# A graph kernel's counting one-hots in sets of four slots, its stream buffers released through ScalarE, its passes begun later

## The chip, the cores and the metric

The kernel runs on one core of a Trainium2 chip. The metric is the time of one execution in microseconds (us) on the device. The kernel before takes 1678.33 us, the median of three runs (1674.64 to 1681.06).

## The reference

12,500 nodes of 128 features pass a layer norm and a ReLU. 200,000 edges, sorted by destination, each bring the row of their source, multiplied by one of four weight matrices (by the edge's type) plus a bias, to their destination; the sums are added to x.

```python
h = jnp.maximum(_layernorm(x, axis=-1), 0.0)
xs = h[src]
msgs = jnp.zeros((xs.shape[0], W.shape[2]), dtype=x.dtype)
for i in range(4):
    mask = (edge_type == i)[:, None]
    msgs = msgs + jnp.where(mask, xs @ W[i] + b[i], 0.0)
out = x + jax.ops.segment_sum(msgs, dst, num_segments=12500)
```

The destinations are drawn so that low-numbered nodes have many edges and most nodes have few.

## The kernel before, in words

**The table.** In the first 190 us the kernel normalizes x and writes h to a table `htab` in DRAM, each row as three bf16 parts of 128 values whose sum is the fp32 value (lines 431 to 514). Row p·98 + j of the table is partition p, column j: `NW` is 98 columns.

**Dense nodes.** The first `C0` = 512 chunks of 128 edges belong to the nodes with many edges. For these the kernel does not fetch rows of h. It counts, for each node and type, how often each of the 12,500 rows occurs, and multiplies the table by these counts. The nodes come in units of three, whose counts share one 32-bit number as three bytes, and the units in batches of `UB` = 27 (18 batches, the first with 17 units).

- *Counting*, `count`, lines 935 to 987. A unit has 2 to 6 *slots*, each of up to 128 edges of one node. In batches 1 to 13 the first three or four units have 6 slots and the others 2; there are 1167 slots, 66 or 70 in most batches. For each slot VectorE (DVE) makes two one-hots, `o1` (128 x 128: which partition, lines 947 or 951) and `o2` (128 x 392: which column and type, line 952), and TensorE (PE) multiplies them into the unit's counts in a PSUM bank `pt` (line 963). After the last slot of a unit ScalarE (ACT) casts the bank into `counts` (line 966). One-hots are made `AHEAD` = 8 slots ahead of their matmul, in 12 buffers of each kind; each matmul waits for its own pair, and each making waits for the matmul that used the buffer last.
- *The pass* over the table, `multiply`, lines 989 to 1040. For each batch the whole table is streamed through SBUF in blocks of `HB` = 4 columns (384 KB, line 997, issued by SyncE, SP), with 4 buffers `hs`. For each column three matmuls (line 1001, one for each bf16 part) add into one PSUM bank `pa`, of which there is a single buffer. At the end ScalarE copies the sums out (`sd`, line 1011), and the next pass may write `pa`. A `tail` of four matmuls with the weights (line 1015) and the adds to the result follow a little later.
- *Their order*, `dense_work`, lines 1062 to 1091. The count of batch b+1 and the pass of batch b are written out side by side: whichever has done the smaller share goes next, and the pass is held as if `BEHIND` = 0.06 further on, so that 4 or 5 slots are counted before its first matmul and its last 6 or 7 columns have no slots beside them. The last pass has no counting beside it.
- `check_sums`, lines 968 to 985, is ten small DVE operations at the end of each count, which verify byte totals; all are issued at once.

**Sparse chunks.** The other 1051 chunks are handled in groups of 16. GpSimd (POOL) fetches their rows of `htab` by indirect DMAs (line 543, into buffers `hm` of the pool `rows`, 18 of them, two chunks each). DVE makes small one-hots `oh` (line 560), PE adds up rows by type (line 577), ScalarE copies the sums (`sb`, line 580), PE applies the weights and counts of biases (lines 595 and 604), and DVE adds the result to a ring of 2048 destination columns (line 665). Filled parts of the ring leave through a PE transpose (line 690), an add to x, fetched by SP (`xo`, line 676), and a store by SP (line 697).

**What sets the order.** The order of instructions on PE, DVE and ACT is that of the program, written out by hand (line 1270). `pace` (lines 1047 to 1057) spreads the dense work evenly over the parts of the sparse groups by TensorE columns. SP and POOL too execute in program order. The framework puts in the waits between engines. A wait that another one already implies is left out: an instruction that waits for a ScalarE copy does not also wait for the PE work that the copy waited for. `held_by` (line 516) adds a wait of one instruction for another by hand.

Of the kernel before, what the change touches and what calls it, by code (L numbers as in the profile page):

```python
# [35 lines left out]
F32 = mybir.dt.float32  # L36
BF16 = mybir.dt.bfloat16
# [5 lines left out]
ALU = mybir.AluOpType  # L43
# [5 lines left out]
P = 128  # L49
# [6 lines left out]
C0 = 512  # L56
UB = 27
MANY = 16
HB = 4
AHEAD = 8  # L60
HOTS = AHEAD + 4
BEHIND = 0.06
RING = 2048
OT = 4
HG = 2
# [8 lines left out]
def kernel(  # L74
# [10 lines left out]
    nc = tc.nc  # L85
# [144 lines left out]
    flag = const.tile([P, 1], I32, name="flag")  # L230

    mid = ExitStack()
    hpool = mid.enter_context(tc.tile_pool(name="rows", bufs=18))
    opool = mid.enter_context(tc.tile_pool(name="onehots", bufs=2))
    spool = mid.enter_context(tc.tile_pool(name="typed", bufs=2))
    x_ps = mid.enter_context(tc.tile_pool(name="x_ps", bufs=4, space=PSUM))
# [279 lines left out]
    def held_by(one, by, reason):  # L516
        tc.add_manual_dep(
            one.ins,
            by.name,
            mybir.DependencyInfo(mybir.DependencyClass.Sync, mybir.DependencyReason.DATA),  # L520
            reason=reason,
        )
# [409 lines left out]
            nc.scalar.copy(acc[:, a:z], pn[:, : z - a])  # L932


    def count(vs, counts):
        todo = []
        for i, u in enumerate(vs):
            of = slots_of(u)
            todo += [(i, c, by, n == 0, n == len(of) - 1) for n, (c, by) in enumerate(of)]
        made = {}  # L940

        def make(k):
            i, s, by, first, last = todo[k]
            o1 = op1.tile([P, P], BF16, name="o1")
            o2 = o2s[:, k % HOTS, :]
            if by == 1.0:
                nc.vector.tensor_scalar(o1, iota_1, loT[:, s : s + 1], None, ALU.is_equal)  # L947
            else:
                if by is None:
                    by = byT[:, (s - PAIRS) // 2 : (s - PAIRS) // 2 + 1]  # L950
                nc.vector.tensor_scalar(o1, iota_1, loT[:, s : s + 1], by, ALU.is_equal, ALU.mult)  # L951
            nc.vector.tensor_scalar(o2[:, :NB], iota_n, hkT[:, s : s + 1], None, ALU.is_equal)  # L952
            made[k] = o1, o2

        done = 0
        for k, (i, s, by, first, last) in enumerate(todo):
            while done < min(k + 1 + AHEAD, len(todo)):
                make(done)
                done += 1
            o1, o2 = made.pop(k)  # L960
            if first:
                pb = x_ps.tile([P, NB + NT], F32, name="pt")
            nc.tensor.matmul(pb, o1, o2, start=first, stop=last)  # L963
            if last:

                nc.scalar.copy(counts[:, :, i * NT : (i + 1) * NT], pb.rearrange("p (b t) -> p b t", t=NT))  # L966
            yield (k + 1) / len(todo)
        def check_sums():
            n = len(vs)
            bi = sdp.tile([P, UB], I32, name="bi")  # L970
            nc.vector.tensor_copy(bi[:, :n], counts[:, NW, : n * NT].rearrange("p (i t) -> p i t", t=NT)[:, :, 0])
            bb = sdp.tile([P, 3, UB], I32, name="bb")
            nc.vector.tensor_single_scalar(bb[:, 0, :n], bi[:, :n], 255, op=ALU.bitwise_and)
            nc.vector.tensor_single_scalar(bb[:, 2, :n], bi[:, :n], 16, op=ALU.arith_shift_right)
            nc.vector.tensor_single_scalar(bi[:, :n], bi[:, :n], 8, op=ALU.arith_shift_right)
            nc.vector.tensor_single_scalar(bb[:, 1, :n], bi[:, :n], 255, op=ALU.bitwise_and)
            bf = sdp.tile([P, 3, UB], F32, name="bf")
            nc.vector.tensor_copy(bf[:, :, :n], bb[:, :, :n])
            top = sdp.tile([P, 2], F32, name="top")
            nc.vector.tensor_reduce(top[:, 0:1], bf[:, :, :n], AX.XY, ALU.max)  # L980
            nc.vector.tensor_reduce(top[:, 1:2], bf[:, :, :n], AX.XY, ALU.add)
            nc.vector.tensor_max(most, most, top[:, 0:1])
            nc.vector.tensor_add(held, held, top[:, 1:2])

        tails.append(check_sums)

    tails = []

    def multiply(vs, counts):
        nu = len(vs)  # L990

        counts = counts.bitcast(F8)
        pa = a_ps.tile([P, 512], F32, name="pa")
        for j0 in range(0, NW, HB):
            j1 = min(j0 + HB, NW)
            hs = hsp.tile([P, HB, D3], BF16, name="hs")
            nc.sync.dma_start(hs[:, : j1 - j0, :], htab.rearrange("(p j) f -> p j f", j=NW)[:, j0:j1, :])
            for j in range(j0, j1):
                of = counts[:, j, : nu * NT * 4].rearrange("p (v m) -> p m v", m=4)[:, :3, :]
                for c in range(3):  # L1000
                    nc.tensor.matmul(  # L1001
                        pa[:, : 3 * nu * NT].rearrange("p (m v) -> p m v", m=3),
                        hs[:, j - j0, c * D : (c + 1) * D],
                        of,
                        start=(j == 0 and c == 0),
                        stop=(j == NW - 1 and c == 2),
                    )
                if j + 1 < NW:
                    yield (j + 1) / NW
        sd = sdp.tile([P, 3 * UB * NT], F32, name="sd")  # L1010
        nc.scalar.activation(sd[:, : 3 * nu * NT], pa[:, : 3 * nu * NT], AF.Copy, scale=512.0)  # L1011
        def tail():
            py = x_ps.tile([P, 3 * UB], F32, name="pt")
            for t in range(NT):
                nc.tensor.matmul(  # L1015
                    py[:, : 3 * nu],
                    wsb[:, t, :],
                    sd[:, : 3 * nu * NT].rearrange("p (v t) -> p v t", t=NT)[:, :, t],
                    start=(t == 0),
                    stop=(t == NT - 1),  # L1020
                )

            def rest():
                for m in range(3):
                    i = 0
                    while i < nu:
                        if vs[i][m] is None:
                            i += 1
                            continue
                        k, d = vs[i][m]  # L1030
                        by = 2 if m < 2 and k == 0 and d >= PAIRS else 1
                        n = next((e for e in range(1, nu - i) if vs[i + e][m] != (k, d + e * by)), nu - i)
                        to = acc[:, d : d + (n - 1) * by + 1 : by]
                        nc.vector.tensor_tensor(to, to, py[:, m * nu + i : m * nu + i + n], ALU.add)
                        i += n

            tails.append(rest)

        tails.append(tail)
        yield 1.0  # L1040
# [201 lines left out]
    counting = mid.enter_context(ExitStack())  # L1242
    dense = counting.enter_context(tc.tile_pool(name="dense", bufs=2))
    sdp = counting.enter_context(tc.tile_pool(name="sdp", bufs=1))
    op1 = counting.enter_context(tc.tile_pool(name="op1", bufs=AHEAD + 4))
    op2 = counting.enter_context(tc.tile_pool(name="op2", bufs=1))
    o2s = op2.tile([P, HOTS, NB + NT], BF16, name="o2")
    nc.vector.memset(o2s[:, :, NB:], 1.0)
    hsp = counting.enter_context(tc.tile_pool(name="hsp", bufs=4))
    raw_sums = outp.tile([P, OT, D], F32, name="xo").rearrange("p j d -> p (j d)")[:, : RAW * G * win_raw]  # L1250
    nc.scalar.copy(raw_sums, raw_py[:, : RAW * G * win_raw])
    raw_adds = [
# [19 lines left out]
    for gi, (t0, g) in list(enumerate(zip(starts, sizes)))[RAW:]:  # L1272
# [16 lines left out]
        for j, part in enumerate(sum_up(t0, g, *now, gi >= FULL)):  # L1289
            late, tails[:] = list(tails), []  # L1290
            while work and spent < pace(gi, part):
                spent = next(work, None)
                if spent is None:
                    work = None
            for f in late:
                f()
            if j == 0:
                if finish:
                    next(finish[0])
                if gi < final:  # L1300
                    oh, made = one_hots_of(starts[gi + 1], sizes[gi + 1])
                    side += made
            if j == when:
                if finish:
                    next(finish.pop(0))
                side.append(lambda: [ending.pop(0)() for _ in list(ending)])
                side += adds
                adds.clear()
                todo = min(todo, len(side) * parts // max(1, parts - 1 - j))
            left = todo * (parts - 1 - j) // parts - (0 if j >= when else todo - len(side))  # L1310
            while side and len(side) > left:
                side.pop(0)()
            for _ in range(2):
                if leaving:
                    leaving.pop(0)()
        assert not side
        if work is None and not dense_out:
            while tails:
                tails.pop(0)()
            dense_out = True  # L1320
            assert goes[0] < gi

# [161 lines left out]
```

## Time and profile before

| | |
|---|---|
| time, median of 3 runs (lowest, highest) | 1678.33 us (1674.64, 1681.06) |
| profiled execution: its time, its span | 1684.81 us, 1683.1 us |
| mean granted TensorE clock in it | 0.95 |
| stretch with counting, passes and sparse groups together | 190 to 1640 us |
| in that stretch: PE busy, DVE, ACT, POOL | 1275.7, 895.2, 330.6, 918.4 us |
| in that stretch: granted clock, DMA share, GB/s | 0.98, 0.65, 192 |
| matmuls of the passes (L1001), counting (L963), sparse (L577) | 5292, 1167, 3009 |

The profile page gives busy times of each engine, the course of the span in 40 slices, the chain of work that ended last, and the costliest groups of instructions by line. PE is TensorE's matmuls and PEld its weight loads beside them; SPq is SyncE's queue; L997 means line 997. Matmuls are pipelined, so the mean length of one in the profile is longer than the distance between two starts. In a group, "<-" and an engine names what ended the idle time before its instructions, and "issue" stands where no event in the profile explains it.

### The profile page before, as it was taken

What the parts mean: (1) busy time and instruction counts of PE and PEld (TensorE: products, weight loads), DVE (VectorE), ACT (ScalarE), POOL (GpSimd) and SP (SyncE); (2) the same over time, 40 slices, a digit from 0 to 9 for tenths busy, and PEclk for the clock granted to TensorE, in tenths of its full rate; (3) what the DMA queues carried; (4) which work ended last, traced back from release to release, by engine and by line L of the source; (5) the groups of instructions that cost most, each with busy time, mean ns of one, the idle gap of its engine ahead of it and who ended that gap; (6) DMA issues with size and microseconds to landing.
All of it is one profiled execution on the core that took longest, in us unless ns stands there. A gap on an engine that the chain in (4) does not pass through costs nothing.

```text
span 1683.1 us, 32652 instructions
## 1 busy us (share of the span) xinstructions
PE 1420.6 (84%) x10984; PEld 926.8 (55%) x10984; DVE 1033.9 (61%) x5305; ACT 445.3 (26%) x1095; POOL 1026.0 (61%) x1078
## 2 busy tenths in 40 slices
PE   3768589898889988888989888988888988898885
PEld 1336366555565556555656555655555555565554
DVE  7880677665766566576647566656654756565244
ACT  5593231222212122212221222122222222222111
POOL 7436666666666566666665666666656666666561
PEclk9875699999999999999999999999999999999997
DMA  7543376766666666666666666666656666666662
GB/s 225 158 155 82 88 233 207 205 199 193 201 190 194 190 196 191 203 193 183 197 194 183 185 196 183 191 201 187 188 165 193 203 187 191 181 194 186 198 185 68
DMA packets 157498, 308.92 MB, mean 184 GB/s; under 512 B 28202, under 2 KB 81116, under 8 KB 157325
## 3 DMA queue, kind: packets, MB, share of 16 engines
q1 hardware_dynamic: 107645, 204.99, 40.3%
q0 software_dynamic: 49680, 101.81, 21.3%
q8 instruction: 86, 1.41, 0.4%
q14 instruction: 87, 0.71, 0.1%
HBM read 290.65 MB, written 16.04 MB: 182 GB/s over the span
## 4 chain that ended last, share of the span: by engine, by line
PE 77%; issue 10%; DVE 5%; another core or an unknown queue 3%; ACT 2%; DMA 2%; SPq 1%; DVEq 0%; ACTq 0%
PE pa L1001 45%; PE pt L963 12%; PE ps L577 7%; PE py L604 6%; PE pt L1015 1%; DMA hs<-htab 1%; PE ps L634 1%; PE py L595 1%; PE pt L690 1%; DVE stt L439 1%; ACT h L460 1%; DVE o L952 1%; DMA hm<-in_x_dram 1%; DVE oh L560 1%
## 5 line engine op out<-in xcount | busy, mean ns | idle before, releaser
L543 POOL DMA_INDIRECT hm<-htab,srcT x1003 | 970.2, 967 | 580.3 <-issue 225.4
L1001 PE MATMUL pa<-counts,hs 128*128 128x324 fp8e4 (+1 forms) x5292 | 976.1, 305 | 112.9 <-issue 95.8
L1001 PEld LDWEIGHTS <-hs 128*128 128x128 bf16 x5292 | 494.2, 97 | 396.0 <-issue 167.9
L963 PE MATMUL pt<-o,o 128*128 128x396 bf16 x1167 | 383.5, 338 | 45.8 <-issue 39.1
L952 DVE TENSOR_SCALAR o<-iota_n,hkT 128x392 bf16<-128x392 f16 x1167 | 386.2, 331 | 14.0 <-PE pa L1001 5.5
L966 ACT CAST counts<-pt 128x396 int32<-128x396 f32 x476 | 229.4, 494 | 506.5 <-PE pt L963 204.4
L560 DVE TENSOR_SCALAR oh<-iota_b,keyT 128x56 bf16<-128x56 bf16 (+8 forms) x1003 | 169.3, 259 | 265.4 <-PE pt L963 88.1
L580 ACT COPY sb<-ps 128x224 f32<-128x224 f32 (+8 forms) x251 | 99.6, 397 | 531.2 <-PE pt L963 182.9
L665 DVE TENSOR_TENSOR ring<-ring,py 128x14 f32 (+7 forms) x976 | 167.5, 172 | 102.5 <-issue 21.5
L577 PE MATMUL ps<-oh,hm 128*128 128x56 bf16 (+8 forms) x3009 | 192.2, 197 | 29.3 <-issue 28.6
L951 DVE TENSOR_SCALAR o<-iota,loT 128x128 bf16<-128x128 bf16 x644 | 169.7, 264 | 75.2 <-PE pt L963 27.8
L577 PEld LDWEIGHTS <-hm 128*128 128x128 bf16 x3009 | 164.7, 98 | 89.5 <-issue 43.7
L951 DVE TENSOR_SCALAR o<-iota,loT,byT 128x128 bf16<-128x128 bf16 x417 | 136.1, 326 | 81.4 <-PE pt L963 40.9
L963 PEld LDWEIGHTS <-o 128*128 128x128 bf16 x1167 | 113.2, 98 | 95.3 <-issue 43.8
L604 PE MATMUL py<-sb,wsb 128*128 128x224 f32 (+7 forms) x488 | 128.6, 404 | 3.5 <-issue 3.2
L604 PEld LDWEIGHTS py<-sb,wsb 128*128 128x128 f32 x488 | 87.3, 191 | 28.5 <-issue 6.8
L527 POOL DMA_INDIRECT hx<-in_x_dram,srcT x48 | 50.2, 1045 | 39.4 <-DVE stt L439 13.9
L599 ACT CAST cnt<-py 128x224 bf16<-128x224 f32 (+7 forms) x61 | 24.0, 394 | 96.4 <-PE pt L963 29.2
L460 ACT ACTIVATE h<-hm,nmrt,rstdt 128x128 f32<-128x128 f32 x98 | 42.8, 495 | 3.5 <-DMA hm<-in_x_dram 2.6
L489 PE MATMUL ps<-h,ident 128*128 128x384 f32 (+1 forms) x34 | 18.1, 618 | 17.7 <-ACT h L460 14.6
L947 DVE TENSOR_SCALAR o<-iota,loT 128x128 bf16<-128x128 bf16 x106 | 26.8, 253 | 8.5 <-remote 4.2
L1015 PE MATMUL pt<-sd,wsb 128*128 128x81 f32 (+1 forms) x144 | 25.4, 334 | 2.7 <-ACT sd L1011 2.7
(234 smaller groups left out, 623.2 us busy)
## 6 DMA issues: line engine op xcount, KB each, us to landing
hs<-htab SPq DMA_DIRECT2D x432, 384.0 KB
hm<-htab,srcT POOLq DMA_INDIRECT x1003
htab<-h SPq DMA_DIRECT2D x32, 288.0 KB
xo<-in_x_dram SPq DMA_DIRECT2D x23, 256.0 KB
out_dram<-xo SPq DMA_DIRECT2D x23, 256.0 KB
hm<-in_x_dram SPq DMA_DIRECT2D x18, 192.0 KB
hs<-htab SPq DMA_DIRECT2D x18, 192.0 KB
hm<-in_x_dram SPq DMA_DIRECT2D x14, 168.0 KB
```

The costliest lines, as they stand in the source:

```text
L460: return nc.scalar.activation(h, xt(k), AF.Relu, bias=nmr[:, k : k + 1], scale=rstd[:, k : k + 1]).ins
L543: one = nc.gpsimd.indirect_dma_start(out=hm[:, (i - h0) * D3 : (i - h0 + 1) * D3], out_offset=None, in_=htab, in_offset=bass.IndirectOffse ...
L560: nc.vector.tensor_scalar(oh[:, i, :], iota_b[:, :K], keyf[:, at : at + 1], None, ALU.is_equal)
L577: nc.tensor.matmul(ps[:, i - i0, :], rows(i, c), oh[:, i, :], start=(c == 0), stop=(c == 2))
L580: nc.scalar.copy(sb[:, i0:i1].rearrange("p g t n -> p g (t n)"), ps[:, : i1 - i0, :])
L604: nc.tensor.matmul(py[:, :g, :], wsb[:, t, :], sb[:, :g, t, :], start=False, stop=(t == NT - 1))
L665: nc.vector.tensor_tensor(to, to, of(i), ALU.add)
L951: nc.vector.tensor_scalar(o1, iota_1, loT[:, s : s + 1], by, ALU.is_equal, ALU.mult)
L952: nc.vector.tensor_scalar(o2[:, :NB], iota_n, hkT[:, s : s + 1], None, ALU.is_equal)
L963: nc.tensor.matmul(pb, o1, o2, start=first, stop=last)
L966: nc.scalar.copy(counts[:, :, i * NT : (i + 1) * NT], pb.rearrange("p (b t) -> p b t", t=NT))
L1001: nc.tensor.matmul(pa[:, : 3 * nu * NT].rearrange("p (m v) -> p m v", m=3), hs[:, j - j0, c * D : (c + 1) * D], of, start=(j == 0 and c == 0),
```

## The change

- One-hots lie in four buffers of four slots each (16 slots instead of 12). A unit's slots are cut into pieces of at most four, and pieces are put together into sets as long as four are not exceeded. PE waits once for a set, at its first matmul, until the last one-hot of the set is made. DVE waits once per set, at its first one-hot, for the last matmul of the set that used the buffer. `o2` is made before `o1`. The sets are made two sets ahead at the start, and then one slot of the set after next for each matmul.
- Blocks of the table's stream have five columns (480 KB) instead of four, in 3 buffers instead of 4, so a pass has 20 blocks instead of 25. The DMA that fills a buffer is held, in addition, by a ScalarE copy of counts: of the copies that were written out after the buffer's last reader and before this DMA, the first. `left_at` keeps the copies with the number of blocks finished when they were written out. With no such copy the framework's wait for PE stays.
- `BEHIND` goes from 0.06 to 0.15.
- The pool `rows` has 16 buffers instead of 18.
- `check_sums` becomes a generator, of which each part of a sparse group takes one step.

```diff
-HB = 4
-AHEAD = 8
-HOTS = AHEAD + 4
-BEHIND = 0.06
+HB = 5
+SLOTS = 4
+SETS = 4
+STREAM = 3
+BEHIND = 0.15
...
-    hpool = mid.enter_context(tc.tile_pool(name="rows", bufs=18))
+    hpool = mid.enter_context(tc.tile_pool(name="rows", bufs=16))
...
+    left_at = []
+    by_blocks = [0]
+    released = []
+
     def count(vs, counts):
...
+            for one in [of[n : n + SLOTS] for n in range(0, len(of), SLOTS)]:
+                if not sets or len(sets[-1]) + len(one) > SLOTS:
+                    sets.append([])
+                sets[-1] += one
+        before = len(released)
+        released.extend(None for _ in sets)
+
+        def make(n):
+            at = before + n
+            o1 = op1.tile([P, SLOTS, P], BF16, name="o1")
+            o2 = o2s[:, at % SETS]
+            for k, (i, s, by, first, last) in enumerate(sets[n]):
+                one = nc.vector.tensor_scalar(o2[:, k, :NB], iota_n, hkT[:, s : s + 1], None, ALU.is_equal)
+                if k == 0 and at >= SETS:
+                    held_by(one, released[at - SETS], "a set of slots has been counted as a whole")
...
+                yield o1[:, k], o2[:, k], one.ins
...
+        for n, of in enumerate(sets):
+            while len(making) < min(n + 3, len(sets)):
+                making.append(make(len(making)))
+                made.append([])
+            for m in range(n, min(n + 2, len(sets))):
+                made[m] += list(making[m])
+            for k, (i, s, by, first, last) in enumerate(of):
+                if n + 2 < len(sets) and len(made[n + 2]) < len(sets[n + 2]):
+                    made[n + 2].append(next(making[n + 2]))
+                o1, o2, _ = made[n][k]
+                if first:
+                    pb = x_ps.tile([P, NB + NT], F32, name="pt")
+                one = nc.tensor.matmul(pb, o1, o2, start=first, stop=last)
+                if k == 0:
+                    held_by(one, made[n][-1][2], "a set of slots is counted when all of it is made")
+                if k == len(of) - 1:
+                    released[before + n] = one.ins
+                if last:
+                    one = nc.scalar.copy(counts[:, :, i * NT : (i + 1) * NT], pb.rearrange("p (b t) -> p b t", t=NT))
+                    left_at.append((by_blocks[0], one.ins))
...
     def multiply(vs, counts):
...
-            nc.sync.dma_start(hs[:, : j1 - j0, :], htab.rearrange("(p j) f -> p j f", j=NW)[:, j0:j1, :])
+            one = nc.sync.dma_start(hs[:, : j1 - j0, :], htab.rearrange("(p j) f -> p j f", j=NW)[:, j0:j1, :])
+            free = [by for n, by in left_at if n > by_blocks[0] - STREAM]
+            if free and by_blocks[0] >= STREAM:
+                held_by(one, free[0], "the buffer of the stream is free")
+            del left_at[: len(left_at) - len(free)]
...
+                if j + 1 == j1:
+                    by_blocks[0] += 1
...
-    op1 = counting.enter_context(tc.tile_pool(name="op1", bufs=AHEAD + 4))
+    op1 = counting.enter_context(tc.tile_pool(name="op1", bufs=SETS))
...
-    o2s = op2.tile([P, HOTS, NB + NT], BF16, name="o2")
-    nc.vector.memset(o2s[:, :, NB:], 1.0)
-    hsp = counting.enter_context(tc.tile_pool(name="hsp", bufs=4))
+    o2s = op2.tile([P, SETS, SLOTS, NB + NT], BF16, name="o2")
+    nc.vector.memset(o2s[:, :, :, NB:], 1.0)
+    hsp = counting.enter_context(tc.tile_pool(name="hsp", bufs=STREAM))
...
+            if checks and next(checks[0], None) is None:
+                checks.pop(0)
```

More of the change, by code (lines that the diff above doesn't have):

```diff
@@ L932, in make_slots @@
             nc.scalar.copy(acc[:, a:z], pn[:, : z - a])
+    left_at = []
+    by_blocks = [0]
+    released = []
     def count(vs, counts):
         todo = []
+        sets = []
         for i, u in enumerate(vs):
             of = slots_of(u)
[L939 to L953, printed above, removed]
@@ L955, in count @@
-        done = 0
-        for k, (i, s, by, first, last) in enumerate(todo):
-            while done < min(k + 1 + AHEAD, len(todo)):
-                make(done)
-                done += 1
[L960 to L967, printed above, removed]
+            of = [(i, c, by, n == 0, n == len(of) - 1) for n, (c, by) in enumerate(of)]
@@ new lines, in count @@
+            todo += of
+            for one in [of[n : n + SLOTS] for n in range(0, len(of), SLOTS)]:
[12 more added lines that the diff above has]
+                    held_by(one, released[at - SETS], "a set of slots has been counted as a whole")
+                if by == 1.0:
+                    one = nc.vector.tensor_scalar(o1[:, k], iota_1, loT[:, s : s + 1], None, ALU.is_equal)
+                else:
+                    if by is None:
+                        by = byT[:, (s - PAIRS) // 2 : (s - PAIRS) // 2 + 1]
+                    one = nc.vector.tensor_scalar(o1[:, k], iota_1, loT[:, s : s + 1], by, ALU.is_equal, ALU.mult)
+                yield o1[:, k], o2[:, k], one.ins
@@ new lines, in count @@
+        making = []
+        made = []
+        done = 0
+        for n, of in enumerate(sets):
[18 more added lines that the diff above has]
+                    left_at.append((by_blocks[0], one.ins))
+                done += 1
+                yield done / len(todo)
+            made[n] = None
@@ L971, in check_sums @@
             nc.vector.tensor_copy(bi[:, :n], counts[:, NW, : n * NT].rearrange("p (i t) -> p i t", t=NT)[:, :, 0])
+            yield True
             bb = sdp.tile([P, 3, UB], I32, name="bb")
@@ L974, in check_sums @@
             nc.vector.tensor_single_scalar(bb[:, 2, :n], bi[:, :n], 16, op=ALU.arith_shift_right)
+            yield True
             nc.vector.tensor_single_scalar(bi[:, :n], bi[:, :n], 8, op=ALU.arith_shift_right)
             nc.vector.tensor_single_scalar(bb[:, 1, :n], bi[:, :n], 255, op=ALU.bitwise_and)
+            yield True
             bf = sdp.tile([P, 3, UB], F32, name="bf")
             nc.vector.tensor_copy(bf[:, :, :n], bb[:, :, :n])
+            yield True
             top = sdp.tile([P, 2], F32, name="top")
@@ L981, in check_sums @@
             nc.vector.tensor_reduce(top[:, 1:2], bf[:, :, :n], AX.XY, ALU.add)
+            yield True
             nc.vector.tensor_max(most, most, top[:, 0:1])
             nc.vector.tensor_add(held, held, top[:, 1:2])
-        tails.append(check_sums)
+        checks.append(check_sums())
     tails = []
+    checks = []
     def multiply(vs, counts):
@@ L1319 @@
                 tails.pop(0)()
+            for check in checks:
+                for _ in check:
+                    pass
             dense_out = True
```

## The prediction

> **What bounds it now.** I read the busy shares and the granted clock first, then the chain that ended last, then the costliest groups.
>
> ```profile
> PE 1420.6 (84%) x10984; PEld 926.8 (55%) x10984; DVE 1033.9 (61%) x5305; ACT 445.3 (26%) x1095; POOL 1026.0 (61%) x1078
> ...
> PEclk9875699999999999999999999999999999999997
> ...
> PE 77%; issue 10%; DVE 5%; another core or an unknown queue 3%; ACT 2%; DMA 2%; SPq 1%; DVEq 0%; ACTq 0%
> ...
> L1001 PE MATMUL pa<-counts,hs 128*128 128x324 fp8e4 (+1 forms) x5292 | 976.1, 305 | 112.9 <-issue 95.8
> L963 PE MATMUL pt<-o,o 128*128 128x396 bf16 x1167 | 383.5, 338 | 45.8 <-issue 39.1
> L952 DVE TENSOR_SCALAR o<-iota_n,hkT 128x392 bf16<-128x392 f16 x1167 | 386.2, 331 | 14.0 <-PE pa L1001 5.5
> ...
> hs<-htab SPq DMA_DIRECT2D x432, 384.0 KB
> ```
>
> TensorE has 84% of the span and 77% of the last chain, so time is won only where it stands. In the dense stretch (190 to 1640 us) starts lie 143 ns apart for L1001 and 166 for L963; a table column (three L1001 with the counting and sparse matmuls between) takes .78 us, one without counting some .61. The waits of PE put 95.8 us before L1001 on "issue". Much of that is at one place per pass, its start. The timeline of one of them (start, length, engine and line; in brackets the idle time before and what ended it):
>
> ```profile
> 721.10 0.59 PE L1001 MATMUL pa<-counts,hs 128*128 128x324 fp8e4 x3
> 721.54 1.00 PE L963 MATMUL pt<-o,o 128*128 128x396 bf16 x5
> ...
> 725.19 0.45 ACT L1011 ACTIVATE sd<-pa 128x324 f32<-128x324 f32 x1
> ...
> 725.68 1.02 PE L1001 MATMUL pa<-counts,hs 128*128 128x324 fp8e4 x6 [3.15 <-issue]
> ```
>
> The old pass ends at 721.7, five slots follow, ScalarE copies the sums out only at 725.2, and the new pass (one `pa`) starts right behind. Over the 16 boundaries with counting, last to first L1001 is 3.59 us in the mean (.9 to 6.9). In each, L1001 follows the copy (.44 us), which starts 2.9 us after the last matmul did. So ScalarE learns late what PE has done: by about 3 us, also in mid-pass (last slot of a unit to its copy: mean 3.1 us, 80% between 1.55 and 4.55). In the before kernel block 0 has landed .3 to 3.8 us before the old pass ends, so the stream costs nothing there.
>
> What a stream block costs when it is waited for shows once in the chain:
>
> ```profile
> 1264.73 0.02 SPq L997
> 1264.75 0.03 issue
> 1264.78 3.84 DMA hs<-htab
> 1268.62 0.47 issue
> 1269.09 0.60 PE pa L1001 x3
> ```
>
> That is 3.8 us for 384 KB; in the mean the packets take 2.76 us and the last signal comes at 3.1. A 192 KB block takes 2.3. On that line 480 KB takes about 3.5 us (estimate).
>
> **The change, part by part.**
>
> *Sets of four slots.* 321 sets replace 1167 single waits of PE on DVE and some 840 of DVE on PE, and about 1000 of PE's 2650 semaphore updates go. PE's price: L1001 with an update starts its successor after 144 ns, without one after 143; so 0. DVE's lead falls from 8–9 slots to 4–8; a set is made in some 4 x 2 x .3 = 2.4 us, against 4 slots x 1.2 us = 4.8 us of PE per set, but DVE learns of a release 2–5 us late, and behind its waiting o2 stand the sparse one-hots (L560) and ring adds, for which L577 waits. Below 0, nothing; above, .05 us on each of 321 sets, 15 us. I take +5.
>
> *Pass starts.* BEHIND .15 puts 10–11 slots ahead of the first matmul instead of 4–5, so 5–6 x .166 = .9 us of counting (and .3 of sparse matmuls) moves into the gap. Against that stands the new hold. When block 0 of a pass is issued, `left_at` is asked for copies made after block B−3 ended. The old count's last copy is emitted near column 83, one block too soon; the first that qualifies is the new count's, and its first unit has 6 slots (batches 1–13; 3–4 after). So blocks 0, 1 and 2 wait on SP for a copy behind six slots and behind the sums' copy on ScalarE: with T0 the old pass's last matmul, 2.9 + .44 + .5 (L966, 494 ns) + .1 to issue = 3.9, then 3.5 to land: first L1001 at T0 + 7.5 against 3.59. Less 1.2 of useful work moved there: +2.7 us x 16 = **+43**. Were ScalarE not late, T0 + 1.3 + .5 + .1 + 3.1 = 5.0 and about +4 in all; with an exposed landing of 4.3, +56. I take 43: the lateness is in every boundary of the trace. Behind SP's hold stand the fetch of `xo` (L676) and the stores (L697), with groups of slack.
>
> *Clock.* Eight of the seventeen boundaries are followed by a slow stretch of 3.4 to 6.8 us. In the windows (start; width, PE, PEld, DVE, ACT and POOL busy, granted clock, DMA share, GB/s):
>
> ```profile
> 726.00:731.00 5.00, 5.00 (x30) 3.43 (x29) 4.60 (x26) 0.49 (x1) 2.97 (x4) 0.66 0.52 153
> 884.00:891.00 7.00, 5.96 (x22) 3.94 (x23) 7.00 (x40) 0.93 (x2) 3.07 (x3) 0.51 0.60 171
> 900.00:1100.00 200.00, 176.94 (x1419) 115.57 (x1417) 125.97 (x645) 46.15 (x110) 127.81 (x133) 0.99 0.65 192
> ```
>
> A stretch at half clock costs at least half of 3.4, 1.7 us. Idle gaps near 6 us should bring it at six more boundaries: **+10** (0 to 15). The Trainium skill (TensorE: Matmul & The Clock Gate, Part 1: The HAM clock gate) gives a window of about 3.4 us in which an idle TensorE falls to half rate; the 0.51 agrees, and by that rule alone every boundary would pay, which adds some 4 us to the sum.
>
> *Block 3 of a pass.* It needs a copy after block 0's end: that of slot 18, emitted at column 10 or 11; it is used at column 15, 4–5 columns or 3.1–3.9 us on. It needs 3.1 (ScalarE) + .5 + .1 + 3.5 = 7.2. Short by up to 3.7 us in the 13 batches with 6-slot units: at most 48, at least .3 x 13 = 4. Half: **+24**, since a pass that began late has PE waiting anyway.
>
> *Other blocks.* Three buffers of five columns are fewer (15 columns, not 16), and a release is seen on the next copy: every two slots, 2.3 us, so 1.16 later in the mean. A block needs 1.16 + 7.2 = 8.4 us from its predecessor's end to its use; two blocks of PE last 2 x 3.88 = 7.76. If strictly so, a block takes 4.18, +.3 us x 14 blocks x 17 passes = 71; if PE's pauses on issue (.1 us in each us) cover it, 0. Today a block's first use is 7.4 us after its issue in the median, so most landings hide with room. I take 40%: **+28**.
>
> *Rest.* `rows` from 18 to 16 buffers: each holds two chunks, so a group of 16 fills half of them instead of 8 of 18; POOL is 61% busy; 0 to 5, taken +2. The check's ten DVE operations (1.9 us a batch) spread over parts: off the path, −5 to 0, taken 0. The column count, matmuls and gathers stay.
>
> **Sum.** 43 + 10 + 5 + 24 + 28 + 2 = +112 us against the profiled execution's 1684.8 (span 1683.1). That run lies 6.5 over the median of 1678.3; I add the difference to the median: **1790 us**. Low ends 4 + 0 + 0 + 4 + 0 − 5 = +3; high ends 56 + 15 + 15 + 48 + 71 + 5 = +210. They will not all fall one way: 1740 to 1850 for this case.
>
> **Rivals.**
> 1. *Only the pass starts pay* (43 + 7): PE's pauses hide the rest. For it: landings hide 7.4 us ahead today. Against: two buffers' time is shorter than the need. 1728 us. Chance .12.
> 2. *The ring of three limits every block:* 43 + 10 + 48 + 71 + 7 = +179, about 1860. For it: the hold is in series with the landing. Against: the 90% of blocks issued over 5.3 us ahead today. .12.
> 3. *Faster:* PE's pauses are the price of its semaphore traffic. If L1001's 95.8 us scale with updates, 1000 of 2650 fewer give −36; more slots in the gaps add 16 x .9 = −14; and fewer long gaps give back some slow stretches. It decides if ScalarE's lateness shrinks with the updates from 3 us to below 1, so that block 0 lands within the gap. With two thirds of it, about 1645. Against: in the last pass, without counting and with half of the updates, the lateness is no shorter (3–5 us), and pauses go on at the same rate:
>
> ```profile
> PE pa L1001 <- issue: 5.7, 9, 1.0
> ```
>
>    (that pass's 66 us; in 1300 to 1500 it is 12.1 in 200). Chance .15. The Trainium skill (same page, "The cost: per-tile semaphore tail") prices each increment at 26.3 ns, one after another: 1000 fewer would be −26 us by it, which speaks for this rival; the 143 and 144 ns above do not show it.
> 4. *It doesn't do what it says:* the hold is never later than the old wait on PE, and gains and losses cancel. Against: block 0 now goes out before the old pass ends and then cannot. 1680 us, .06.
>
> The forecast has .55. About 0.5% (8 us) is what a measurement can tell from no change. Faster .15 (rival 3), the same .06, slower .79. The range, 1660 to 1880, leaves out half of rival 3 and the top of rival 2.
>
> **What would show it.** Pass boundaries near 7.5 us with L1001 waiting on DMA hs, not on the sums' copy; SP's L997 waiting on ACT L966; blocks 0–2 issued together behind the first copy of a batch; a wait at column 15; more windows near 0.5. Wrong if block 0 lands before the sums are copied, if the lateness of PE's signals falls with their number (then boundaries near 5 us), or if L1001's issue pauses shrink by a third.

## The result, and the profile after

The changed kernel takes 1745.21 us (median of 4, 1744.29 to 1748.43) beside 1676.49 us of the kernel before (median of 4): a ratio of 1.041, 95% interval 1.038 to 1.044, or +69 us. The profiled execution took 1744.29 us, its span is 1742.5. Lines move: the passes' matmuls are L1040, counting L985, the copy of counts L991, the stream's DMA L1032, the copy of the sums L1052. From the page of the changed kernel:

```profile
PE 1435.4 (82%) x10984; PEld 938.3 (54%) x10984; DVE 1015.9 (58%) x5305; ACT 450.0 (26%) x1095; POOL 1031.1 (59%) x1078
...
PEclk8976799998999899999999999999999899999997
...
PE 52%; issue 19%; DMA 14%; DVE 5%; another core or an unknown queue 4%; ACT 4%; SPq 2%; DVEq 0%; ACTq 0%
...
L1040 PE MATMUL pa<-counts,hs 128*128 128x324 fp8e4 (+1 forms) x5292 | 970.4, 309 | 195.1 <-DMA hs<-htab 150.7
...
hs<-htab SPq DMA_DIRECT2D x342, 480.0 KB
```

The work is the same, and PE's busy time nearly so. What is new is DMA: 14% of the chain instead of 2%, and 150.7 us of idle time before the passes' matmuls end with a block of the table, where before the largest releaser was "issue" with 95.8. The waits of PE and of SP's queue say the same from both ends (what waited, releaser, total, times, longest), first in the kernel before, then in the changed kernel:

```profile
PE pa L1001 <- issue: 95.8, 143, 4.6
...
PE pa L1001 <- DMA hs<-htab: 1.9, 3, 0.9
...
SPq L997 <- PE pt L963: 420.3, 150, 8.2
```
```profile
PE pa L1040 <- DMA hs<-htab: 150.7, 88, 8.1
PE pa L1040 <- issue: 40.3, 46, 4.6
...
SPq L1032 <- ACT counts L991: 633.3, 146, 12.1
```

SP now waits mostly for the copies of counts, where it waited for PE. But look at the lines on issue: while waits for blocks rose from 1.9 to 150.7 us, the pauses on issue fell from 95.8 to 40.3. This is the puzzle of the case.

The start of the same pass as in the prediction, in the changed kernel's timeline:

```profile
748.05 0.59 PE L1040 MATMUL pa<-counts,hs 128*128 128x324 fp8e4 x3
748.48 1.67 PE L985 MATMUL pt<-o,o 128*128 128x396 bf16 x9
...
749.74 0.44 ACT L1052 ACTIVATE sd<-pa 128x324 f32<-128x324 f32 x1 [0.36 <-PE pt L985]
...
750.51 0.49 ACT L991 CAST counts<-pt 128x396 int32<-128x396 f32 x1 [0.32 <-PE pt L985]
751.02 1.27 SPq L1032 DMA_DIRECT2D hs<-htab  x3
755.26 0.99 PE L1040 MATMUL pa<-counts,hs 128*128 128x324 fp8e4 x3 [4.60 <-issue]
```

Three DMAs go out together right behind the first copy of the new count, and PE starts 4.2 us after the first of them. The bracket on the last line says "issue", not DMA: the releaser is a guess from events, and the order of the lines tells more than the label. Column 15 of another pass:

```profile
601.64 0.49 ACT L991 CAST counts<-pt 128x396 int32<-128x396 f32 x1 [5.62 <-PE ps L578]
...
602.16 1.06 SPq L1032 DMA_DIRECT2D hs<-htab  x2
...
605.46 0.74 PE L1040 MATMUL pa<-counts,hs 128*128 128x324 fp8e4 x4 [2.70 <-DMA hs<-htab]
```

ScalarE stands idle for 5.6 us before the copy that lets block 3 go; the block is needed before it can have landed.

Two windows, over the start of one pass and of another (columns as in the prediction; the granted clock is third from the end):

```profile
588.00:593.00 5.00, 4.39 (x18) 3.11 (x19) 3.76 (x21) 0.49 (x1) 0.96 (x1) 0.50 0.54 213
1353.00:1358.00 5.00, 5.00 (x25) 3.76 (x26) 2.04 (x17) 0.00 (x0) 1.38 (x2) 0.50 0.75 258
```

PE counts as fully busy in the second and starts only 25 matmuls in 5 us: at half clock two L1040 start 269 ns apart instead of 143.

### The profile page after: what moved, and what is told of

Its sections match the earlier page's. It is cut to its first block, busy times and chain, and to the rows that moved or that the text cites. A ratio compares the mean times of both kernels' runs of the same rounds, so it can differ in the third digit from the quotient of the medians.

```text
span 1742.5 us, 32539 instructions
## 1 busy us (share of the span) xinstructions
PE 1435.4 (82%) x10984; PEld 938.3 (54%) x10984; DVE 1015.9 (58%) x5305; ACT 450.0 (26%) x1095; POOL 1031.1 (59%) x1078
## 4 chain that ended last, share of the span: by engine, by line
PE 52%; issue 19%; DMA 14%; DVE 5%; another core or an unknown queue 4%; ACT 4%; SPq 2%; DVEq 0%; ACTq 0%
PE pa L1040 27%; DMA hs<-htab 14%; PE pt L985 8%; PE py L605 5%; PE ps L578 4%; ACT counts L991 2%; PE pt L1056 2%; SPq L1032 1%; PE ps L635 1%; DVE oh L561 1%; PE py L596 1%; PE pt L691 1%; DVE o L967 1%; ACT sb L581 1%
## 5 line engine op out<-in xcount | busy, mean ns | idle before, releaser
L1040 PE MATMUL pa<-counts,hs 128*128 128x324 fp8e4 (+1 forms) x5292 | 970.4, 309 | 195.1 <-DMA hs<-htab 150.7
L1040 PEld LDWEIGHTS <-hs 128*128 128x128 bf16 x5292 | 490.9, 98 | 478.1 <-DMA hs<-htab 187.3
L959 DVE TENSOR_SCALAR o<-iota_n,hkT 128x392 bf16<-128x392 f16 x1167 | 381.3, 327 | 97.7 <-PE pt L985 44.1
L985 PE MATMUL pt<-o,o 128*128 128x396 bf16 x1167 | 374.9, 345 | 23.2 <-issue 10.4
L991 ACT CAST counts<-pt 128x396 int32<-128x396 f32 x476 | 230.0, 493 | 555.8 <-PE pt L985 306.3
L666 DVE TENSOR_TENSOR ring<-ring,py 128x14 f32 (+7 forms) x976 | 171.2, 175 | 82.5 <-PE py L605 20.8
L967 DVE TENSOR_SCALAR o<-iota,loT 128x128 bf16<-128x128 bf16 x644 | 175.2, 272 | 0.0
L985 PEld LDWEIGHTS <-o 128*128 128x128 bf16 x1167 | 114.0, 99 | 77.3 <-issue 23.9
L967 DVE TENSOR_SCALAR o<-iota,loT,byT 128x128 bf16<-128x128 bf16 x417 | 139.6, 335 | 0.0
L1000 DVE COPY bi<-counts 128x27 int32<-128x27 int32 (+1 forms) x18 | 4.2, 232 | 106.0 <-issue 62.0
L1056 PEld LDWEIGHTS pt<-sd,wsb 128*128 128x128 f32 x144 | 31.3, 304 | 6.9 <-ACT sd L1052 4.8
L1056 PE MATMUL pt<-sd,wsb 128*128 128x81 f32 (+1 forms) x144 | 31.0, 379 | 4.7 <-ACT sd L1052 4.7
```

The source lines that it names most:

```text
L666: nc.vector.tensor_tensor(to, to, of(i), ALU.add)
L959: one = nc.vector.tensor_scalar(o2[:, k, :NB], iota_n, hkT[:, s : s + 1], None, ALU.is_equal)
L967: one = nc.vector.tensor_scalar(o1[:, k], iota_1, loT[:, s : s + 1], by, ALU.is_equal, ALU.mult)
L985: one = nc.tensor.matmul(pb, o1, o2, start=first, stop=last)
L991: one = nc.scalar.copy(counts[:, :, i * NT : (i + 1) * NT], pb.rearrange("p (b t) -> p b t", t=NT))
L1040: nc.tensor.matmul(pa[:, : 3 * nu * NT].rearrange("p (m v) -> p m v", m=3), hs[:, j - j0, c * D : (c + 1) * D], of, start=(j == 0 and c == 0),
```

## The experiments

Theory A, mine: the hold starves the stream at the start of each pass and at column 15; PE's pauses on issue are of another origin, and are covered while PE waits for blocks. Theory B: the sets of four took the pauses away, since PE waits and signals less, and the hold costs even more than the difference shows.

The runs fell on different chips, on which the kernel before itself takes different times, so every ratio is against it on the same chip. On two chips it takes 1405 us (e1 to e4, e8 to e11). There ScalarE copies the sums .34 us after a pass's last matmul in nearly all passes, and PE hardly pauses. On a third it takes 1707 to 1709 us (e5 to e7, e12). There ScalarE learns late and PE pauses, as in the two profiles above, whose chip (1676 us) was of this kind. I call them prompt chips and late chips. The times expected for e1 to e4 were written for a chip like the first; they are read here as ratios to its 1676 us.

**e1: no hold.** The changed kernel without these two lines:

```diff
-            if free and by_blocks[0] >= STREAM:
-                held_by(one, free[0], "the buffer of the stream is free")
```


> The changed kernel without the hold of stream DMAs on ScalarE's copies; they wait for TensorE's last reader of the buffer, as before. Theory A (the hold starves the stream; TensorE's pauses on issue, which are shorter in the changed kernel, are only covered by the waits for blocks and come back without them): boundaries near 3 us, no column-15 wait, pauses on issue back to some 130 to 150 us, time 1665 to 1690. Theory B (the sets of four took the pauses away, and the hold costs more than the difference shows): boundaries and block waits go as in A, the pauses stay low (near 50 us), time 1580 to 1620.


Measured (prompt chip): 1418.8 us, ratio 1.010 (1.008 to 1.012). Waits for blocks are 4.5 us in all. Theory A's times are a ratio of .993 to 1.008 and theory B's .94 to .97, so the result lies just above A. But on the pauses, about which the two differ, this chip says nothing, having hardly any.

**e2: the sets alone**, on the kernel before. The edit is shown against the changed kernel; the check is also issued all at once again, and `rows` keeps 16 buffers.

```diff
-HB = 5
+HB = 4
-STREAM = 3
+STREAM = 4
-BEHIND = 0.15
+BEHIND = 0.06
...
-                held_by(one, free[0], "the buffer of the stream is free")
```


> The kernel before with the sets of four slots alone (and 16 instead of 18 row buffers, for room). Blocks of four columns in four buffers, passes begun at 0.06, no hold. Theory A: 1670 to 1690, pauses on issue as before. Theory B: the pauses fall by two thirds, 1580 to 1620.


Measured (prompt chip): 1409.66 us, ratio 1.004 (1.003 to 1.006). The sets win nothing. The ratio lies within theory A's .996 to 1.008, but this chip has no pauses that could fall. PE waits 12.0 us for the last one-hot of a set, where it waits 5.3 us for single one-hots in e11, whose counting is that of the kernel before:

```profile
PE pt L985 <- DVE o L967: 12.0, 11, 3.3
```

**e3: the hold alone**, in the kernel before.

```diff
+                left_at.append((by_blocks[0], one.ins))
...
+            free = [by for n, by in left_at if n > by_blocks[0] - STREAM]
+            if free and by_blocks[0] >= STREAM:
+                held_by(one, free[0], "the buffer of the stream is free")
```


> The kernel before with the hold alone, with its four buffers of four columns. With 4 or 5 slots ahead of a pass no copy of the new batch is written out before block 0, so pass starts are not held. Theory A: a block in mid-pass needs 1.2 + 3.1 + 0.6 + 3.1 = 8.0 us where three blocks of PE last 9.3: 1675 to 1700. Theory B, in which fewer updates of TensorE shorten its pauses: 1640 to 1665, as stream matmuls lose many of theirs.


Measured (prompt chip): 1474.17 us, ratio 1.049 (1.048 to 1.051). Both expectations failed (ratios of 1.00 to 1.01 and .98 to .99). Block 0 indeed goes out early and the starts stay at 1.4 us; but blocks 1 to 3 then wait for the first copy of the new count, and block 1 goes out 3.1 us after the old pass's last matmul in the mean. Column 4, where block 1 begins, loses 25.7 us over the passes, and blocks 4, 6 and 8 another 24 (gaps counted as further down). I had thought of block 0 only. A bunch of slots without a copy hurts wherever it meets a hold.

**e4: more slots ahead alone**, in the kernel before.

```diff
-BEHIND = 0.06
+BEHIND = 0.15
```


> The kernel before with BEHIND 0.15 alone: 10 to 11 slots ahead of a pass, and some 15 columns at its end without. Both theories: 16 gaps filled by 0.9 us more, so 1655 to 1680; if slots ahead only delay the copy of the sums, no difference.


Measured (prompt chip): 1410.95 us, ratio 1.005 (1.003 to 1.007), a small loss where a ratio of .987 to 1.002 was expected. Starts grow from 1.4 us (e3, e10) to 3.10, by more than the 6 x .166 us of the slots moved: where ScalarE is prompt, there is no gap to fill.

**e5: the changed kernel again.**


> The changed kernel as it is, once more, since the four experiments before came from a chip on which the kernel before takes 1405 us and ScalarE copies the sums .34 us after the pass's last matmul. If this call's chip is such a one: starts at 2.0 + .5 + 3.5 = 6 us after the old pass instead of 3.4 without the hold, +41 us; column 15 some +25, clock +10: ratio to before 1.05 to 1.07. If ScalarE is late by 3 us here: ratio 1.04 as in the first measurement.


Measured (late chip): 1779.37 us, ratio 1.040 (1.034 to 1.046): the first result again, 72 us. Starts take 7.69 us in the mean, and column 15 loses 36.8 us.

**e6: the hold from block 4 on.**

```diff
-            if free and by_blocks[0] >= STREAM:
+            if free and by_blocks[0] >= STREAM and j0 >= 4 * HB:
```


> The changed kernel with the hold only from block 4 of a pass on; blocks 0 to 3 wait for TensorE alone. The theory that the pass starts and column 15 carry the loss: boundaries as without any hold, no column-15 wait, ratio 1.01 to 1.02 where ScalarE is not late (need 1.2 + .9 + .1 + 3.5 = 5.7 us in a window of two blocks, over 6.5), 1.01 to 1.04 where it is late by 3 us. The rival, that every block of the ring pays: within .01 of the changed kernel's ratio.


**e7: e1's kernel, beside them.**


> The changed kernel without any hold, beside the other two on one chip. Where ScalarE is not late: ratio 1.01 as in e1. Where it is late, theory A (pauses on issue come back): ratio 1.00 to 1.01; theory B (the sets took them away): .94 to .97.


Measured (late chip): e6 1705.41 us, ratio 1.000 (.997 to 1.002); e7 1699.65 us, ratio .996 (.994 to .998). Freeing blocks 0 to 3 takes the whole loss away; e6 comes out below the 1.01 to 1.04 that I expected on such a chip. And these two, 6 us apart, answer the puzzle. Waits of PE, first e6, then e7:

```profile
PE pa L1040 <- DMA hs<-htab: 84.7, 68, 3.1
PE pa L1040 <- issue: 54.3, 80, 3.7
PE ps L578 <- issue: 22.9, 41, 1.2
PE pt L985 <- issue: 22.5, 22, 3.7
```
```profile
PE pa L1038 <- issue: 82.3, 145, 3.1
PE ps L578 <- issue: 37.1, 62, 3.2
PE pt L985 <- issue: 20.0, 32, 3.5
...
PE pa L1038 <- DMA hs<-htab: 14.5, 18, 1.9
```

By these lines e6 waits 70 us longer for blocks, while its three rows on issue hold 40 us less. By the gaps between PE's starts, counted as further down, it is 88 us more of waiting and 77 us less of pauses (158 to 81), and the stretch from the first to the last pass matmul is 11.5 us longer in these two profiles; the medians differ by 6 us. Both count in the same sets, so it isn't the sets that shorten the pauses: e7, with 321 waits of PE on DVE instead of 1167, pauses as much as the kernel before did on the first chip (158 us against 137). Theory B falls. A rival remains to be named: with the hold fewer of PE's matmuls have to signal, 1473 semaphore updates in e6 against 1728 in e7. But from the kernel before, with 2649, to e7 they fell by a third and the pauses didn't, though on two different chips. A pause seems to fall due only where PE would otherwise run on, and a wait to take its place; that is an inference from these totals.

**e8: the hold on blocks 0 to 2 alone.**

```diff
-            if free and by_blocks[0] >= STREAM:
+            if free and by_blocks[0] >= STREAM and j0 < 3 * HB:
```


> The changed kernel with the hold on blocks 0 to 2 of each pass alone: the complement of e6, without the hold at column 15 too. If starts and column 15 add up separately and ScalarE is late on this chip: ratio to before 1.025 to 1.035 (starts +58 us and slow clock, less the .4% that the rest wins). If the starts are all: 1.04. If they only move the wait to the next block: below 1.01. Where ScalarE is not late: 1.03 to 1.05.


Measured (prompt chip): 1487.14 us, ratio 1.059 (1.057 to 1.060), above my range. The start of the same pass:

```profile
635.89 0.60 PE L1040 MATMUL pa<-counts,hs 128*128 128x324 fp8e4 x3
...
637.53 0.49 ACT L991 CAST counts<-pt 128x396 int32<-128x396 f32 x1 [0.57 <-PE pt L985]
...
638.05 1.28 SPq L1032 DMA_DIRECT2D hs<-htab  x3
642.51 0.61 PE L1040 MATMUL pa<-counts,hs 128*128 128x324 fp8e4 x3 [4.00 <-DMA hs<-htab]
```

ScalarE is prompt here, and the start still takes 6.24 us in the mean, against 3.42 in e1: 45 us over 16 passes. The hold costs without any lateness. My range left out the clock: 55 us lie at half clock here and 10 in e1; counted by the matmuls that start there, some 15 us.

**e9: sets and more slots ahead, four columns in four buffers, no hold.** The edit is against the changed kernel.

```diff
-HB = 5
+HB = 4
-STREAM = 3
+STREAM = 4
...
-                held_by(one, free[0], "the buffer of the stream is free")
```


> The sets and passes begun at 0.15, but blocks of four columns in four buffers and no hold. Without the hold the changed kernel still waits some 15 to 20 us for blocks where ScalarE is late; four buffers should take two thirds of that back: ratio .985 to .995 there, 1.005 to 1.01 where it is not late (e2 and e4 gave 1.004 and 1.005 each). If sets or slots ahead save nothing where ScalarE is late: 1.00.


**e10: five columns in three buffers alone**, in the kernel before.

```diff
-HB = 4
+HB = 5
-    hsp = counting.enter_context(tc.tile_pool(name="hsp", bufs=4))
+    hsp = counting.enter_context(tc.tile_pool(name="hsp", bufs=3))
```


> The kernel before with blocks of five columns in three buffers alone. A block is needed two blocks (7.8 us) after its buffer came free, and 2.4 us of lateness plus 3.6 to land fit where the lateness is at its mean: ratio 1.000 to 1.010 where ScalarE and SP learn late, 1.000 to 1.004 where not.


Measured (prompt chip): e9 1413.53 us, ratio 1.006 (1.004 to 1.007); e10 1407.98 us, ratio 1.002 (1.001 to 1.003). Alone, sets, slots ahead and blocks of five cost .4, .5 and .2% there. Sets and slots ahead together cost .6% in e9, and all three 1.0% in e1, so the prices don't simply add. None of them gains. The question that e9 was meant for, what it wins on a late chip, stays open.

**e11: two banks for the sums**, in the kernel before, to test that a pass waits for the copy of the sums.

```diff
-    x_ps = mid.enter_context(tc.tile_pool(name="x_ps", bufs=4, space=PSUM))
+    x_ps = mid.enter_context(tc.tile_pool(name="x_ps", bufs=3, space=PSUM))
...
-    a_ps = mid.enter_context(tc.tile_pool(name="a_ps", bufs=1, space=PSUM))
+    a_ps = mid.enter_context(tc.tile_pool(name="a_ps", bufs=2, space=PSUM))
```


> The kernel before with two banks for a pass's sums and three instead of four for counts, so that a pass need not wait for ScalarE's copy of the sums. If the boundaries of 3.59 us are that wait: they fall below 1.5 us where ScalarE is late, 35 to 60 us, ratio .965 to .98, less what three banks of counts cost; where it is not late, .995 to 1.00. If the boundary is something else (block 0, or the counts): 1.00.


Measured (prompt chip): 1405.18 us, ratio 1.000 (.999 to 1.001). Only the last start shortens, from .83 (e10) to .14 us. It says nothing about a late chip.

**e12: e8, with the copy of the sums among the releasing copies.**

```diff
-        nc.scalar.activation(sd[:, : 3 * nu * NT], pa[:, : 3 * nu * NT], AF.Copy, scale=512.0)
+        one = nc.scalar.activation(sd[:, : 3 * nu * NT], pa[:, : 3 * nu * NT], AF.Copy, scale=512.0)
+        left_at.append((by_blocks[0], one.ins))
```


> The kernel of e8 (hold on blocks 0 to 2 of a pass alone), with the copy of the old pass's sums entered among the copies that release the stream. Blocks 0 to 2 then wait for this copy, not for that of the new count's sixth slot. If the place of the releasing copy sets the starts: where ScalarE is not late, block 0 goes out at .34 + .44 + .1 = .9 us instead of 2.0 to 2.1, the first matmul at 4.7 to 5.2 instead of 6.24 in the mean, and the ratio falls from 1.059 to 1.035 to 1.045; where it is late, the start is at 2.9 + .5 + 3.5 = 7 us instead of 7.7, ratio 1.02 to 1.03. If the three blocks that are issued at once are what is slow: no change at either.


Measured (late chip): 1726.16 us, ratio 1.011 (1.008 to 1.014). The start falls to 6.79 us, as expected, and the three DMAs now follow the copy of the sums:

```profile
738.23 0.44 ACT L1052 ACTIVATE sd<-pa 128x324 f32<-128x324 f32 x1 [0.39 <-PE pt L985]
738.69 1.27 SPq L1032 DMA_DIRECT2D hs<-htab  x3
...
742.23 0.60 PE L1040 MATMUL pa<-counts,hs 128*128 128x324 fp8e4 x3 [2.92 <-DMA hs<-htab]
```

The ratio is below what I expected. The starts are 2.4 us longer than e7's, 39 us over 16 passes, and the kernel is 26 us slower: here too PE pauses less (62.4 us before pass matmuls, not 82.3). Since e8 ran on a prompt chip, the start is to be compared with the changed kernel's 7.69 us in e5, on this chip.

## Why the prediction was right, and where it was not

Slower was right, for the reason given, and the size was too large: +69 instead of +112, so that 1745 lies at the lower end of the forecast's own range (1740 to 1850). The terms, in the profiles of the first pair; gaps here are those over .45 us between PE's starts, less .2 each. At the first column of a block they count as waits for blocks, away from the starts of passes and blocks as pauses:

| term | predicted | found |
|---|---|---|
| 16 starts, less the work moved there | +43 | 3.59 to 7.79 us: +67 − 19 = +48 |
| clock | +10 | matmuls of passes and counting at half clock, 179 to 336: about +21 |
| column 15 (block 3) | +24 | +27 |
| other blocks | +28 | 9.5 to 92.4 us: +83 |
| PE's pauses | within the line above | 137 to 42 us: −95 |
| sets, rows, check | +7 | not separable on this chip; sets +.4% on a prompt one |

The found terms add to +84, and the stretch from the first to the last pass matmul grew by 64 us. The 20 us between them are not assigned; a slow stretch or a pause that lies inside a wait would be counted twice. The split also depends on what is taken off a gap: with .35 each, other blocks and pauses are +74 and −72. Either way the two nearly cancel.

*Pass starts* were nearly right in their parts: block 0 goes out 4.00 us after the old pass's last matmul (3.9 predicted) and PE starts 3.79 after that (3.5 predicted). The prediction took its 3.5 from a block of 384 KB that it said shows once in the chain, at 3.84 us; the chain of the kernel before has four more, in its first pass, of 4.08 to 4.87 us. Whether the three blocks that go out together slow each other was not tested. In one point the picture was off, and that the sum came out all the same is luck: the sums' copy starts after 2.0 us in the mean, not 2.9, and the copy of counts doesn't follow at once but is late by itself, at 3.5 us. e6 against e5 (1705 and 1779 us on one chip) shows that blocks 0 to 3 carry the loss, and e12 against e5 (starts of 6.79 and 7.69 us) that an earlier releasing copy shortens the start.

*Clock.* I added six boundaries at half clock; all seventeen have it within 9 us of the first matmul (eight before), and on average longer. The Trainium skill (TensorE: Matmul & The Clock Gate, Part 1: The HAM clock gate) says that an idle window of about 3.4 us drops TensorE to half rate. With starts of 7.8 us the trace agrees: 0.50 in the windows above. I should have let every boundary pay.

*The other blocks* are the step that failed: "if PE's pauses on issue cover it, 0 ... I take 40%". Their waits came, at more than the full size (+83 against 71), but PE's pauses shrank by about as much. e6 beside e7 gives the price: 70 to 88 us more of waiting for blocks, 6 us more of time. The cover that I allowed for was nearly whole, so 0 to 6 us would have been right instead of 28. Of the 48 us between the forecast's +112 and the stretch's 64, this term is 40 (28 against 83 − 95 = −12). One sign that the prediction named as showing it wrong also came: L1001's pauses on issue were to keep two thirds of their 95.8 us and fell to 40.3. The rival that this sign was meant for, fewer signals, is hardly the reason: e7 has 1728 updates instead of 2649, and there they are 82.3.

*Sets.* Bounded at 0 to 15, taken at +5: e2 gives +5 us on a prompt chip. The rival that fewer signals would win 26 to 36 us had one place to show itself, e7 against the kernel before on a late chip: −7.6 us in all. Filling longer gaps with six more slots each, my −14 of rival 3, could explain a gain of that size; I have not measured the parts there. The rule of the Trainium skill (TensorE: Matmul & The Clock Gate, The cost: per-tile semaphore tail), 26.3 ns for each increment, is not seen in any run here. In e2, on a prompt chip, PE has 1820 updates instead of 2649, and the kernel is 5 us slower.

The rival "only the pass starts pay" (1728 us) came closest in mechanism: starts, column 15 and the clock pay, the rest is covered.

Only the version without the hold ran on both kinds of chip: it is .4% faster than the kernel before on the late one and 1.0% slower on a prompt one. No version was faster than before on a prompt chip, and the changed kernel itself was not run there.

## What to carry to other kernels

If a wait is moved from the engine that frees a buffer to another one that works on it later, list the first uses after every change of phase: here the new releaser did not exist until six slots into the next batch, and on the late chip that cost 4% while the same hold in mid-pass cost .4%. A stall on a chain with pauses of its own need not add to them, as the two cancelled here: price it by an experiment that has both, as e6 and e7, and not by the sum of its waits.

## What the runs showed of the hardware that I had not expected

The same kernel takes 1405 us on two chips and 1676 to 1709 on others, with the same 143 ns between matmuls, and clocks of .975 and .95. Part of the difference is in pauses of PE that no wait explains (137 us in the profile before, under 10 in e2, e10 and e11), and part in how soon ScalarE acts on PE's signal: .34 us after the last matmul in nearly every pass, or .3 to 6.4. Against e11, the nearest kernel profiled on a prompt chip, the profile before is 280 us longer: 44 us before the first pass matmul, and 230 from there to the last, of which the pauses are 130 and the starts of passes some 39. The rest is not assigned, and no run here shows why chips differ.
